# First half's exponentials, convolution order, six experts in halves, and ten constants of an instruction planner

## The chip, the core and the metric

The kernel runs on one core of one Trainium2 chip. The core has five engines that work side by side and meet only through semaphores: TensorE (matrix products, PE in the profile), VectorE (DVE), ScalarE (ACT, which evaluates functions from a loaded table), GpSimd (POOL), and SyncE (SP), which here issues all transfers. The metric is device time in microseconds. Before the change the median of three runs is 1351.64 us (1351.54 to 1353.74).

## The reference

Eight sequences of 512 tokens with 128 channels go through four residual blocks, each behind a layer norm. All is in fp32.

```
x = x + mamba(norm(x))      # projection, 3-tap convolution, silu, decay scan over 512 steps, projection
x = x + moe(norm(x))        # 8 experts, all computed, weighted by a softmax router
x = x + attention(norm(x))  # 16 heads, chunk mask with 25 columns of left context
x = x + moe(norm(x))        # the same weights again
```

The scan block computes, per token, `delta = clip(softplus(dt))`, `decay = clip(exp(-delta * a))`, `drive = (1 - decay) * tanh(b) * xb`, and then `state = decay * state + drive`, `y = sum(state * tanh(c)) + D * xb`. Its other half of the channels, `zb`, passes by the scan. An expert computes `(silu(x Wg) * (x Wu)) Wd` with an inner width of 512.

## The kernel before

**Work and tiles.** Tokens are the free axis, so a sequence is a tile of 128 x 512. The bulk of the work is the expert stream `ffn_stream` (sequence after sequence, expert after expert, four blocks `f` of 128 inner columns each). For each block there are the products `g`, `u` (into one PSUM bank each), the silu of `g`, the product `h`, its split into two parts `hs` of reduced-precision fp32, and the down products `y`. Each product is made of three matmuls over those parts (`matmul3`). The kernel names tiles as in the trace: `xt` and `tp` are the transposed and normalised input, `lps`, `rps`, `cps` the router, `cwb` the spread expert weights, `mh`, `mv`, `mxb`, `mzb`, `mbc`, `mde`, `mdec`, `mst`, `mcx`, `mo` the steps of the scan block in order, `acc` the experts' sum (and, as `macc`, `delta` of the scan block).

**The order.** Nothing of the order is left to a scheduler on the chip. A planner in the same file (classes `Clock`, `Lanes`, `Engine`) walks through Python generators while it builds the program, keeps an estimated end time for each engine, and emits the instructions one by one; each engine then runs its own in that order. The expert stream goes on whenever its inputs and a PSUM bank are free; the other work (scan block of later sequences, router, attention) sits in lanes that are slipped in between. The constants decide when: `SIDE`, `JOIN`, `JOIN_MAX` are the time that a ready piece of TensorE work is held back so that it can go together with another one, `PRESS`, `SECOND`, `FIRST` are advantages in the choice of the next lane, `MAMBA_DUE`, `PREP_DUE`, `LATE` say from which position of the stream a lane counts as late, `WARM_GAP` and `WARM_TO` rule the filler products below.

**The start.** The stream can't begin before sequence 0 has gone through the whole scan block. So this sequence is done in two halves of 256 tokens (`first_halves`): `half(c)` does the convolution and the silu, `scanned(c)` the rest. Within it run the lanes `rows` (tanh, spread products), `inputs`, `decays` (exponentials, which need another ScalarE table than silu and tanh), `clips`, `steps` (scan). In the kernel before, `decays` waits until both halves have had their tanh and silu (`issued["tanh"] == 2`), so the table is changed once for both. `undisturbed` holds the second half's VectorE work while the first half's norm is under way (`"quiet" in done`). `mamba_consts` prepares weights; its last part (`wxz`, and `route_consts`) waits for `"halves" in done`. The expert weights arrive at the same time: ScalarE casts each (`wg`, `wu`, `wd`), GpSimd makes the low part.

**Halves of experts.** For sequence 0, `passes` puts the first `SPLIT` experts on the first half of the tokens, then the same experts on the second half, and the rest on whole sequences. A half product has 256 columns and two `f` blocks share one bank.

**Filler.** While TensorE has nothing to do, the planner emits products that nobody reads: `warm` before the stream, `idle` in it (`keep_warm`, up to position `WARM_TO` of the stream, counted in sequences). An `idle` product takes a PSUM bank from the stream's pool and gives it back.

Of the kernel before, what the change touches and what calls it, by code (L numbers as in the profile page):

```python
# [93 lines left out]
AHEAD = 0.2  # L94
EDGE = 0.1
FIRST = 0.6
LATE = 0.3
SIDE = 0.5
JOIN = 2.0
JOIN_DUE = 0.0  # L100
JOIN_MAX = 6.0
JOIN_ATT = 3.0
JOIN_END = 2.0
MOST = 6
OTHERS = 4
AT_FIRST = 7
WARM = 3.5
WARM_GAP = 0.25
WARM_TO = 1.5
SECOND = 0.2  # L110
PRESS = 0.4
HELD = 0.18
MAMBA_DUE = 0.9
PREP_DUE = 0.9
ATT_LEAD = 2.5
EARLY = 5
SPLIT = 4
EARLIEST = 2 * (DEPTH + 1)


# [257 lines left out]
def block_kernel(ctx: ExitStack, tc: tile.TileContext, x, pack_a, pack_b, pack_c, w_qkv, mask, mask_t, w_o,  # L378
# [24 lines left out]
    done = {}  # L403
# [30 lines left out]
    def freed(t, who="others"):  # L434

        held[who] -= 1
        lanes.give("bank", t + TO_PE)
        return t
# [134 lines left out]
    def mamba_consts(sb, mc):  # L573
        table("natural_log_exp_and_others", 6)

        pick = sb.tile([P, L], F32, tag="dec", name="pick", bufs=5)[:, : 2 * DSTATE]
        pool.tensor_tensor(pick, ident[:, : 2 * DSTATE], ident[:, 32 : 32 + 2 * DSTATE], ALU.add)
        sel = sb.tile([P, 2 * NSTEP, 2, INNER], F32R, name="sel", bufs=1)
        for m in range(2):
            rows = pick[:, m * DSTATE : m * DSTATE + DSTATE].rearrange("p (s i) -> p i s", s=2)  # L580
            pool.tensor_copy(
                sel[:, m * NSTEP : m * NSTEP + NSTEP], rows[:, :, :, None].to_broadcast([P, NSTEP, 2, INNER])
            )
        mc["sel"] = sel.rearrange("p n s c -> p n (s c)")
        yield "A", pa_there

        nega = sb.tile([P, NSTEP], F32, name="nega", bufs=1)
        alog = pa[:, A_ALOG : A_ALOG + NSTEP]
        sp_ = sb.tile([P, NSTEP], F32, tag="sp_a", name="sp_a", bufs=1)
        act.activation(sp_, alog, AF.Abs)  # L590
        act.activation(sp_, sp_, AF.Exp, scale=-1.0)
        act.activation(sp_, sp_, AF.Ln, bias=1.0)
        win = [sb.tile([P, P], F32R, name=f"win_{i}", bufs=1) for i in range(2)]
        src = pa[:, A_WIN : A_WIN + P]
        act.copy(win[0], src)
        yield "V"
        dve.scalar_tensor_tensor(sp_, alog, 0.0, sp_, ALU.max, ALU.add)
        dve.tensor_scalar(nega, sp_, 1e-4, -1.0, ALU.add, ALU.mult)
        dve.tensor_tensor(win[1], src, win[0].bitcast(F32), ALU.subtract)
        mc["win"] = win  # L600
        yield "A"

        cap = sb.tile([P, NSTEP], F32, name="cap", bufs=1)
        act.activation(cap, nega, AF.Exp, scale=1e-4)
        table("silu_and_others", 18)

        yield "T", pc_there
        wp = yield from side([P, P], "wdt_ps")
        pe.matmul(wp, pc[:, 0:P], pc[:, P : 2 * P], start=True, stop=True)
        wdt = sb.tile([P, P], F32, name="wdt", bufs=1)  # L610
        yield "A"
        freed(act.copy(wdt, wp))
        mc["wdt"] = wdt

        wbc = sb.tile([P, P], F32, name="wbc", bufs=1)
        yield "P"
        for h in range(2):
            pool.tensor_copy(
                wbc[INNER * h : INNER * h + INNER].rearrange("p (c n) -> p c n", c=4),
                pa[:INNER, None, A_PBC : A_PBC + 32].to_broadcast([INNER, 4, 32]),  # L620
            )
        mc["wbc"] = wbc
        yield "V"
        dve.tensor_scalar(cap, cap, 1.0, None, ALU.min)
        mc["nega"], mc["cap"] = nega, cap

        yield lambda: "halves" in done
        yield "AV"
        wxz = sb.tile([P, P], F32, name="wxz", bufs=1)
        act.activation(wxz[:INNER], pa[:INNER, A_WOUT : A_WOUT + P], AF.Copy, scale=pa[:INNER, A_D : A_D + 1])  # L630
        mc["wxz"] = wxz, act.copy(wxz[INNER:], pa[INNER:, A_WOUT + P : A_WOUT + 2 * P])
        route_consts()
# [72 lines left out]
    def first_halves(sb, consts, h, xo):  # L705
# [9 lines left out]
        issued = {"tanh": 0}  # L715
        add = first, second

        def half(c):
            cs = slice(c * HALF, c * HALF + HALF)
            v, xb = vs[c], xbs[c]  # L720
            yield "A"
            act.activation(v, h[:, cs], AF.Copy, scale=kc[1])
            yield "V"
            n = 1 - c
            dve.scalar_tensor_tensor(
                v[:, n:], h[:, cs.start + n - 1 : cs.stop - 1], kc[0], v[:, n:], ALU.mult, ALU.add
            )
            yield "V"
            e = dve.scalar_tensor_tensor(
                v[:, : HALF - c], h[:, cs.start + 1 : cs.stop + n], kc[2], v[:, : HALF - c], ALU.mult, ALU.add  # L730
            )
            if c:
                freed(e)
            yield "A"

            act.activation(xb[0:INNER], v[0:INNER], AF.Silu)
            there2 = act.activation(xb[INNER:P], v[0:INNER], AF.Silu)
            yield "T", there2
            pde, pbc = yield from sides(([P, HALF], f"mde0_{c}"), ([P, L], f"mbc0_{c}"))
            pbc = pbc[:, :HALF]  # L740
            pe.matmul(pbc, consts["wbc"][:INNER], xb[:INNER], start=True, stop=True)
            pe.matmul(pde, consts["wdt"][INNER:], xb[INNER:], start=True, stop=True)
            add[c](scanned(c, pbc, pde))

        def scanned(c, pbc, pde):
# [3 lines left out]
            def rows():  # L749
                yield "A"  # L750
                bc = sb.tile([P, L], F32R, tag="bc", name=f"mbc0_{c}")[:, :HALF]
                act.activation(bc, pbc, AF.Tanh)
                act.activation(pbc[32:64], pbc[32:64], AF.Tanh)
                there["z"] = act.activation(zb, vs[c], AF.Silu)
                issued["tanh"] += 1
                yield "V"
                e = freed(dve.tensor_tensor(bc[32:64], pbc[32:64], bc[32:64].bitcast(F32), ALU.subtract))
                for m, into in enumerate((bxs, ccs)):
                    if m:
                        yield lambda: issued["tanh"] == 2  # L760
                    for p in range(2):
                        yield "T", e
                        t = yield from side([P, 2, HALF], f"m{'bc'[m]}x0_{c}_{p}")
                        for i in range(2):
                            into["t", p] = spread(t[:, i], consts, bc, 2 * p + i, m)
                        into[p] = t
# [16 lines left out]
            def decays():  # L783
                yield "V"

                e = freed(dve.tensor_scalar(delta, pde, bdt, LN_E_1, ALU.add, ALU.min))
                yield lambda: issued["tanh"] == 2
                yield "A", e
                nega = consts["nega"]
                table("natural_log_exp_and_others", 6)  # L790
                act.activation(delta, delta, AF.Exp)
                act.activation(delta, delta, AF.Ln, bias=1.0)
                for p in range(2):
                    yield "A"
                    dec = sb.tile([P, 2, HALF], F32, tag="dec", name=f"mdec0_{c}_{p}", bufs=5)
                    for i in range(2):

                        decs["t", p, i] = act.activation(
                            dec[:, i], delta, AF.Exp, scale=nega[:, 2 * p + i : 2 * p + i + 1]
                        )  # L800
                    decs[p] = dec
                if c:
                    table("exp_and_others", 0)
# [53 lines left out]
            for p in range(2):  # L857
                yield lambda: p in scans
                yield from undisturbed()
                yield "V", max(scans[p][1], ccs["t", p])  # L860
                cx = sb.tile([P, 2, HALF], F32, tag="acc", name=f"mcx0_{c}_{p}")
                e = freed(dve.tensor_tensor(cx, ccs[p], scans[p][0], ALU.mult))
                yield "T", e
                for t in range(2):
                    for i in range(2):
                        pe.matmul(
                            ops[t], cx[:, i, t * P : (t + 1) * P], pa[:, A_WOUT : A_WOUT + P],
                            start=False, stop=(p == i == 1),
                        )
            yield "V"  # L870
            part = xo[0][:, 2 * c : 2 * c + 2]
            for t in range(2):
# [150 lines left out]
    def ffn_prep(k, b, xc, t0=0, nt=NT):  # L1023
# [42 lines left out]

        yield lambda: clock.table in TABLES[AF.Exp] or pos[0] >= k * B + b - LATE
        yield "A"
# [351 lines left out]
    def attention(sb):  # L1420
# [62 lines left out]
        def scores(s, both):  # L1483

            qs, ks, _ = loaded[s]
            for m in range(NPAIR):
                for h in range(2):
                    rows = slice(64 * h, 64 * h + QROWS)
                    for i, (q, k) in enumerate(blocks(steps[s][1])):
# [4 lines left out]
                        )  # L1494
            lanes.add(maxima(s, both, e), joins=JOIN_MAX)

# [364 lines left out]
```

## Time and profile before

| | |
|---|---|
| median of three runs | 1351.64 us |
| profiled execution | 1351.62 us, of it a span of 1349.8 us |
| TensorE busy | 1328.9 us |
| VectorE, ScalarE, GpSimd busy | 1036.8, 964.7, 940.4 us |
| first product `g` of the expert stream | 34.31 us after the span's start |
| `ACT_TABLE_LOAD` | 109 records, 1283 ns each |
| mean granted TensorE clock | 0.996 |

The page gives busy times of engines over the span, then a picture of the span in 40 slices, the chain that ended last, and groups of instructions. A line of the timeline has start and duration in us, the engine, the operation with its output and inputs, a count where several were merged, and in brackets how long the engine had been idle and what ended that. A line of the table by stretches has the length of the stretch and then busy time and instruction count of PE, PEld (weight loads), DVE, ACT and POOL, then the granted TensorE clock (1.00 is full), and the share and rate of the transfers. TensorE products are pipelined, so one record is longer than the distance from its start to the next one's.

### The profile page before, as it was taken

To read this page: it belongs to the slowest core of one execution; us is meant where nothing else is said; L and a number is where in the kernel's file an instruction comes from. 1 tells how busy PE (TensorE), PEld (TensorE's weight loads), DVE (VectorE), ACT (ScalarE), POOL (GpSimd) and SP (SyncE) were. 2 spreads that over 40 slices of the span, in tenths; PEclk is the share of its full clock that TensorE was granted. 3 is DMA by queue.
4 is the path that set the end of the run, shared out by engine and by line. 5 is a ranking of instruction groups with operands and counts; after the bars stand their busy time and mean duration, and the time that the engine had idled before them with its cause. 6 is when DMAs were issued, how large, how long until landed. Compare 5 with 4: busy or idle time off the path is not lost.

```text
span 1349.8 us, 29533 instructions
## 1 busy us (share of the span) xinstructions
PE 1328.9 (98%) x10261; PEld 1053.3 (78%) x10261; DVE 1036.8 (77%) x3114; ACT 964.7 (71%) x1694; POOL 940.4 (70%) x1042
## 2 busy tenths in 40 slices
PE   7999999999999999999999999999999999999998
PEld 7877778788788877777777777777777777778887
DVE  6887888688888867898788887888888787855443
ACT  7768576867787556777777777777877767765654
POOL 5877576776767757666766767767677676777776
PEclk9999999999999999999999999999999999999999
DMA  3321304232112242344345444454544434222111
GB/s 126 95 72 38 87 24 101 62 81 73 45 48 56 63 85 54 73 97 118 79 103 111 99 106 100 104 109 89 118 91 104 119 71 88 61 69 55 40 40 40
DMA packets 230861, 107.75 MB, mean 80 GB/s; under 512 B 86417, under 2 KB 226616, under 8 KB 230712
## 3 DMA queue, kind: packets, MB, share of 16 engines
q1 hardware_dynamic: 230712, 105.87, 33.9%
q8 instruction: 81, 1.33, 0.4%
q14 instruction: 68, 0.56, 0.1%
HBM read 77.64 MB, written 27.79 MB: 78 GB/s over the span
## 4 chain that ended last, share of the span: by engine, by line
PE 89%; POOL 3%; ACT 3%; issue 3%; DVE 2%; DMA 0%; POOLq 0%; DVEq 0%
PE u L269 25%; PE y L269 25%; PE g L269 25%; PE ao L269 2%; PE aw L269 2%; PE as L269 2%; POOL h L269 1%; PE mo L269 1%; PE aqk L269 1%; ACT h L269 1%; DVE h L269 1%; PE mde L269 1%; PE aout L269 1%; PE yp L269 1%; ACT L269 1%
## 5 line engine op out<-in xcount | busy, mean ns | idle before, releaser
L269 POOL TENSOR_TENSOR h<-h,h 128x512 fp32r<-128x512 f32 x492 | 640.0, 1310 | 279.0 <-ACT h L269 219.4
L269 PE MATMUL u<-xt_f,wu 128*128 128x512 f32 (+1 forms) x1584 | 451.5, 395 | 3.5 <-ACT h L269 2.7
L269 PE MATMUL g<-xt_f,wg 128*128 128x512 f32 (+1 forms) x1584 | 448.3, 393 | 2.1 <-ACT h L269 1.9
L269 PE MATMUL y<-h,wd 128*128 128x512 f32 (+1 forms) x1584 | 445.5, 392 | 1.4 <-POOL h L269 0.8
L269 DVE TENSOR_TENSOR h<-u,h 128x512 f32<-128x512 f32 x420 | 285.9, 686 | 157.5 <-PE u L269 109.3
L269 ACT ACTIVATE h<-g 128x512 f32<-128x512 f32 x512 | 303.4, 597 | 123.2 <-PE g L269 100.1
L269 ACT CAST h<-h 128x512 fp32r<-128x512 f32 x437 | 268.4, 619 | 171.2 <-DVE h L269 169.6
L269 PEld LDWEIGHTS g<-xt_f,wg 128*128 128x128 f32 x1584 | 288.5, 189 | 70.3 <-ACT h L269 3.0
L269 PEld LDWEIGHTS y<-h,wd 128*128 128x128 f32 x1584 | 288.3, 188 | 70.2 <-POOL h L269 1.4
L269 PEld LDWEIGHTS u<-xt_f,wu 128*128 128x128 f32 x1584 | 286.6, 189 | 71.7 <-ACT h L269 4.1
L269 POOL TENSOR_TENSOR acc<-acc,cwb 128x512 f32<-128x512 f32 (+1 forms) x114 | 148.0, 1298 | 52.5 <-DVE cwb L269 33.8
L269 ACT ACT_TABLE_LOAD x109 | 139.8, 1283 | 24.7 <-PE g L269 23.2
L269 DVE CUSTOM_DVE_ANT_0 amasked<-as,maskq 128x60 f32<-128x60 f32 x640 | 95.4, 213 | 5.0 <-PE as L269 4.8
L269 DVE TENSOR_TENSOR cwb<-y,cwb 128x512 f32<-128x512 f32 (+1 forms) x116 | 77.5, 668 | 16.0 <-PE y L269 14.4
L269 DVE TENSOR_TENSOR apt<-aw,maskk 125x400 f32<-125x400 f32 (+2 forms) x160 | 88.1, 570 | 0.0
L269 DVE SCALAR_TENSOR_TENSOR h<-h,g 128x512 f32<-128x512 f32 x92 | 62.3, 681 | 27.0 <-ACT h L269 26.6
L269 ACT ACTIVATE apt<-apt 125x400 f32<-125x400 f32 (+2 forms) x160 | 81.5, 540 | 0.4
L269 DVE SCALAR_TENSOR_TENSOR h<-u,h 128x512 f32<-128x512 f32 x92 | 62.6, 683 | 3.3 <-PE g L269 0.5
L269 DVE DVE_READ_ACCUMULATOR2_ANT amx<- 128x1 f32 x640 | 52.1, 81 | 0.0
L269 DVE CAST h<-h 128x512 fp32r<-128x512 f32 x75 | 48.8, 651 | 1.2
L269 DVE COPY v<-avr 125x128 f32<-125x128 f32 (+2 forms) x40 | 25.7, 644 | 26.4 <-PE ao L269 26.4
L269 PEld LDWEIGHTS ao<-apt,v 125*32 125x32 f32 (+2 forms) x1280 | 27.4, 109 | 14.6 <-DVE h L269 4.4
(205 smaller groups left out, 1239.5 us busy)
## 6 DMA issues: line engine op xcount, KB each, us to landing
cwb<-cwd_f SPq DMA_DIRECT2D x124, 256.0 KB
aqd<-apc SPq DMA_DIRECT2D x32, 192.0 KB
ks<-aqd SPq DMA_DIRECT2D x48, 93.8 KB
x_fo<-x SPq DMA_DIRECT2D x16, 256.0 KB
aqd<-apc SPq DMA_DIRECT2D x32, 128.0 KB
x_f<-x SPq DMA_DIRECT2D x15, 256.0 KB
qs<-aqd SPq DMA_DIRECT2D x48, 75.0 KB
aod<-aos SPq DMA_DIRECT2D x24, 100.0 KB
```

Source lines behind the costliest of these rows:

```text
L269: f(*args, **kw)
```

## The change

The exponentials of half `c` now wait only for this half's tanh and silu. The second half's convolution on VectorE is emitted after the first's. The late constants wait for `"rows"`, which is set when a half has emitted its tanh and silu. The quiet phase, which holds back the second half's VectorE work, is opened already when the first half's output products have been emitted. `SPLIT` goes from 4 to 6, and ten constants of the planner get other values. Since the planner reads these, the order of the whole program is planned anew.

```diff
-LATE = 0.3
-SIDE = 0.5
-JOIN = 2.0
+LATE = 0.4
+SIDE = 0.6
+JOIN = 3.5
-JOIN_MAX = 6.0
+JOIN_MAX = 8.0
-WARM_GAP = 0.25
-WARM_TO = 1.5
-SECOND = 0.2
-PRESS = 0.4
+WARM_GAP = 0.15
+WARM_TO = 2.5
+SECOND = 0.1
+PRESS = 0.2
-MAMBA_DUE = 0.9
-PREP_DUE = 0.9
+MAMBA_DUE = 1.1
+PREP_DUE = 0.7
-SPLIT = 4
+SPLIT = 6
...
-        yield lambda: "halves" in done
+        yield lambda: "rows" in done
         yield "AV"
         wxz = sb.tile([P, P], F32, name="wxz", bufs=1)
...
             act.activation(v, h[:, cs], AF.Copy, scale=kc[1])
             yield "V"
+            if c:
+                yield lambda: "conv" in issued
+                yield "V"
             n = 1 - c
...
             if c:
                 freed(e)
+            issued["conv"] = 1
             yield "A"
...
                 issued["tanh"] += 1
+                done["rows"] = 0.0
                 yield "V"
...
                     if m:
-                        yield lambda: issued["tanh"] == 2
+                        yield lambda: issued["tanh"] > c
...
                 e = freed(dve.tensor_scalar(delta, pde, bdt, LN_E_1, ALU.add, ALU.min))
-                yield lambda: issued["tanh"] == 2
+                yield lambda: issued["tanh"] > c
                 yield "A", e
...
+            if c == 0:
+                done["quiet"] = 0.0
             yield "V"
             part = xo[0][:, 2 * c : 2 * c + 2]
```

## The prediction

> **What bounds the kernel now.** I read the page first. TensorE is busy for 98% of the span and carries 89% of the chain that ended last, in equal parts for g, u and y: the expert stream.
>
> ```profile
> span 1349.8 us, 29533 instructions
> PE 1328.9 (98%) x10261; PEld 1053.3 (78%) x10261; DVE 1036.8 (77%) x3114; ACT 964.7 (71%) x1694; POOL 940.4 (70%) x1042
> ...
> PE 89%; POOL 3%; ACT 3%; issue 3%; DVE 2%; DMA 0%; POOLq 0%; DVEq 0%
> ```
>
> So time can only come from three places: the 34.31 us before the first g, the waits inside the stream, and work added to or taken from TensorE. The timeline of the start shows the first. The change of tables at 17.67 stands behind the second half's silu (mzb), the exponentials (macc) begin 1.30 us later, and the first half's transposed input (xt_f) is copied at 32.36.
>
> ```profile
> 14.59 0.40 ACT L269 ACTIVATE mzb<-mv 128x256 f32<-128x256 f32 x1
> 17.25 0.40 ACT L269 ACTIVATE mzb<-mv 128x256 f32<-128x256 f32 x1
> 17.67 1.28 ACT L569 ACT_TABLE_LOAD   x1
> 18.97 0.87 ACT L269 ACTIVATE macc<-macc 128x256 f32<-128x256 f32 x2
> 32.36 0.37 ACT L269 CAST xt_f<-tp_f 128x256 fp32r<-128x256 f32 x1 [2.85 <-PE tp_f L269]
> 34.31 0.77 PEld L269 LDWEIGHTS g<-xt_f,wg 128*128 128x128 f32 x6 [0.26 <-PE idle L269]
> ```
>
> TensorE's timeline in the stream shows the second. Filler (idle) hides part of the waits: five of them fill 68.38 to 70.58, 0.44 us apart, because each waits for the bank of the one before.
>
> ```profile
> 67.25 0.27 PE L269 MATMUL cps_f<-ident,cw_f 128*16 128x128 f32 x1
> 68.38 2.14 PE L269 MATMUL idle<-sel 128*128 128x256 f32 x5 [0.86 <-DVE cwt_f L269]
> 70.58 1.46 PE L269 MATMUL u<-xt_f,wu 128*128 128x256 f32 x6
> ...
> 176.60 1.64 PE L269 MATMUL g<-xt_f,wg 128*128 128x512 f32 x3 [1.94 <-ACT h L269]
> ```
>
> The table by stretches adds what such a wait costs afterwards: the next 3.4 us run at half the clock, which is 1.7 us of work lost. In the stream this happens twice.
>
> ```profile
> 67.40:70.90 3.50, 2.35 (x9) 1.25 (x8) 3.45 (x12) 3.45 (x5) 0.97 (x2) 0.99 0.02 4
> 70.90:74.30 3.40, 3.40 (x15) 3.01 (x14) 2.44 (x7) 3.39 (x8) 2.70 (x5) 0.51 0.26 75
> 173.30:176.70 3.40, 1.46 (x7) 0.85 (x5) 1.25 (x3) 3.37 (x6) 2.25 (x2) 0.99 0.15 38
> 176.70:180.10 3.40, 3.40 (x8) 2.71 (x9) 2.37 (x4) 2.06 (x4) 1.86 (x2) 0.51 0.17 39
> ```
>
> In both, ScalarE is full (3.45 of 3.50, 3.37 of 3.40): it changes tables and makes decays while TensorE waits for a silu to free a bank.
>
> The sum is made against the profiled execution, 1351.62 us (span 1349.8 and 1.8 around it), practically the median of 1351.64.
>
> **A. The start, up to the first g.** The instruction order of the changed program tells what moves; rows of before give durations.
> ScalarE: the two wxz copies (9.56 to 10.27) move from before the convolution to behind mzb; mh ends at 9.91, so the convolution's first copy goes from 10.30 to 9.95, and all of half 0 with it (0.35). The convolution's order on VectorE and ScalarE is the same in both programs: that edit moves nothing. The first mzb then ends at 14.64, wxz at 15.3, the table load (1.30) at 16.6: the first exponentials come 2.4 us earlier than 18.97. But ScalarE then has in its queue: macc 0.87, decays 1.71, a load back 1.30, the second half's silus 0.84, 0.82 until its tanh (TensorE products between, filled by a weight cast), tanh and mzb 1.1, six weight casts or small copies 2.2, a load 1.3, macc 0.9, decays and two casts 2.8, a load 1.3. Two loads are new. That is 31.8 for the xt copy instead of 32.36; the router and the two products mo follow (0.41 and 0.71), and the filler at 33.95 before g is gone: g at 33.5, **-0.8 us**. VectorE and GpSimd would allow earlier: mcx of half 0 ends at 24.5 (26.89 less 2.4), the norm's power waits on GpSimd behind three weight parts to 28.9, tp ends at 30.0. So the 2.4 us become 0.8, because ScalarE is next late. Bounds: -2.4 (ScalarE not in the way) and +1.0 (one more wait of the kind before macc).
>
> The Trainium skill, "ScalarE: Activation LUTs", section "What ACT_TABLE_LOAD costs", puts a switch at 1.28 us plus a drain of about 1.38, 2.66 in all, and so speaks against this change. The row decides: the next activation starts 1.30 us after the load. By the page the three loads behind 16.6 would put xt 4.1 us later, and the whole sum at about 1352.
>
> **B. From g to the end of expert 3's first half.** A common mark is the product mde of sequence 1, with the same 15.1 us of expert products before it in both orders; before, it starts at 57.05. The quiet phase now holds back the second half on VectorE: in the old order two mbx products and two clips (0.69, 0.41, 0.69, 0.90) ran before the xt part at 33.04; in the new one all of it comes after. From 32.98: mbx 0.69 twice, a copy 0.27, clips to 35.4 (they wait for GpSimd's 1.3 us part, as the 0.90 us clip at 29.48 did), scans 1.37 each, two mcx 0.68, with silu steps between. mcx ends at 40.6 and 44.5, against 37.47 and 39.67. Behind them in TensorE's queue stand mo, then cps (0.27, GpSimd's weight at 46.1), then the fourth g: at about 46.3 instead of 41.97. Allowing for what was reordered, expert 2's first u is 4.5 us behind. Then the old order has what the new one lacks: seven more filler products there (14 against 7), standing for 0.4, 1.0 and 1.1 us of waiting at 45, 51.7 and 56.0, and small ones. The new chain goes over GpSimd's parts (h of expert 1 at 52.6) and seven groups of 0.72 to mde at 57.4, or over the convolution and silu to 55.9. I take the later, 57.3: **A and B together +0.2 us**. Bounds: -1.2 and +4.5 (nothing caught up).
>
> **C. From there to sequence 1** (before: g at 129.06). I sum the waits of before: 3.2 (67.3 to 70.6), 1.7 half clock, 1.1, 0.75, 0.55, 0.9, and about 1.5 in small ones at 117 to 129: 9.7 us, of which 14 fillers at 0.31 (9.25 us for 30 in the stream) are 4.3. Between two silus of the stream ScalarE has at most so much other work, priced by rows (copy 0.53, decay 0.65, load 1.30): before 5.9, 7.0, 5.5 and 6.4 us, in the new order once 8.2 (six experts in halves put sequence 1's decays and the router's exponential under one pair of loads; from the mark on the old order has eight loads, the new one four with the pair on the border to sequence 1). So: again 14 fillers, 4.3; other waits 3.7 x 8.2/24.8 = 1.2; one half clock with even chance 0.85. Sum 6.4, **-3.3 us**. Bounds: -6 (no half clock, short fillers) and +2 (a wait of 8.2 less the 5 that pass unnoticed, with a half clock).
>
> **D. Later sequences.** Waits of before: 1.6 at 150, 1.94 and 1.7 (half clock) at 175, 1.45 at 264, 0.7 at 521, 0.84 at the end: 8.3 us. ScalarE's gaps over 5.6 us number five before and eight after, the largest 7.0 and 7.2. Filler now goes on to position 2.5, which keeps the clock up in a wait like that at 175 but costs 0.12 to 0.44 each. I take half of one half clock away, **-0.9**; bounds -4 and +4, since the new order's waits can't be read from the old trace.
>
> The Trainium skill, "TensorE: Matmul & The Clock Gate", section "HAM oscillation — how this bites in real kernels", asks only for no TensorE gaps above about 3.4 us. Here a wait of 1.94 us, busy 1.46 in the window, was enough. By the page D would hold no half clock at all, and its -0.9 would be -1.7.
>
> **E. TensorE's own work.** 144 products of 256 columns replace 72 of 512: 12 of them take 1.44 us (61.75 to 63.19 on TensorE), 0.12 each, and three of 512 columns 0.70 (704.74 to 705.44), 0.23 each. 144 x 0.120 - 72 x 0.2315 = **+0.6 us**. The products slipped into the stream leave it 261 times instead of 273; two more of the small transposes of attention go with a neighbour, which the rows price at 0.08 each: **-0.2** (0 to -1). The four extra transfers and GpSimd additions lie beside the stream.
>
> Sum: +0.2 - 3.3 - 0.9 + 0.6 - 0.2 = -3.6: **1348.0 us**.
>
> **Rivals.**
> *R1, VectorE's late second half is never made up* (slower). Place: TensorE's queue at mo, 37 to 50 us. For it: the 4.5 us behind, and VectorE busy for 8.9 of the 10 us from 40 to 50, so it has little to catch up with. Against it: the gaps of before that follow. Price: +4.5 for B and a half clock of 1.7: 1351.6 + 4.5 + 1.7 - 3.3 - 0.9 + 0.4 = 1354.0, and 1357.3 where C gains nothing; the middle is 1355.5. It decides when mde starts later than about 61.
> *R2, the waits only move.* For it: 33 fillers against 30, ScalarE's gaps over 5.6 add up alike. C and D are 0: 1351.6 + 0.2 + 0.4 = 1352.2, or 1350 with the start's bound. The early exponentials do not do what they say, since ScalarE meets the same 31.8.
> *R3, both half clocks and half of the later waits go.* C -6, D -4: 1351.6 + 0.2 - 10 + 0.4 = 1342.
>
> **How the numbers follow.** Forecast 0.52 (own range 1344 to 1351.5; about 0.7 of it below 1348.9), R1 0.22, R2 0.10, R3 0.16. A difference below 0.2% (2.7 us) can't be told from none. Faster: 0.36 + 0.16 + 0.02 = 0.54; same 0.21; slower 0.25. The range leaves a tenth at each side: half of R3 below 1342, half of R1 above 1355.5.
>
> **What would show it.** In the changed kernel: a table load near 15.3 and exponentials near 16.6; xt_f's copy right behind a load near 31.9, g near 33.5 (A); TensorE waiting for DVE mcx near 38 to 45, mde near 57 (B); one long ScalarE run before expert 5 with fillers and perhaps a clock of 0.5, and g of sequence 1 near 126 (C). I am wrong if g of sequence 1 starts after 129, or if waits beyond 130 us add up to more than 12 us.

## The result and the profile after

The changed kernel takes 1368.65 us (median of five, 1364.74 to 1369.59) against 1351.54 (1350.17 to 1353.74) before: the ratio is 1.0119, with an interval of 1.0101 to 1.0137. It is 17 us slower. The forecast was 1348.0, its range ended at 1355.5. The profiled execution of the changed kernel took 1364.74 us, the least of the five, so the two traces differ by 13.2 us of span (1363.0 against 1349.8); the sums below are made against that, and some 4 us of the loss are in no trace.

The head of the page and the chain that ended last, of the changed kernel:

```profile
span 1363.0 us, 29691 instructions
...
PE 1336.1 (98%) x10328; PEld 1059.4 (78%) x10328; DVE 1036.8 (76%) x3103; ACT 964.3 (71%) x1708; POOL 942.0 (69%) x1046
...
PE 85%; ACT 5%; DVE 4%; DMA 2%; issue 1%; POOL 1%; SPq 1%; POOLq 0%; DVEq 0%; ACTq 0%
```

All engines are busy for as long as before to within 0.7%. What changed is the chain: 85% of it is TensorE instead of 89%, and transfers, 0% before, have 2%. Of the 13.2 us TensorE counts as idle for 6.0 and as busy for 7.2; fillers that stand in a wait and products at half the clock also count as busy, so the page alone doesn't separate waiting from work. The timeline of the start shows that the time didn't go there:

```profile
15.55 1.28 ACT L569 ACT_TABLE_LOAD   x1
16.85 0.86 ACT L269 ACTIVATE macc<-macc 128x256 f32<-128x256 f32 x2
...
32.12 0.37 ACT L269 CAST xt_f<-tp_f 128x256 fp32r<-128x256 f32 x1
33.60 0.78 PEld L269 LDWEIGHTS g<-xt_f,wg 128*128 128x128 f32 x6
33.63 0.96 PE L269 MATMUL g<-xt_f,wg 128*128 128x256 f32 x6
```

The load was forecast for 15.3, the exponentials for 16.6, the copy for 31.8 and the first g for 33.5. The list of what TensorE waited for (in total, times, longest, from the first g to the end) shows some of the new waits; the first fence is the changed kernel, the second the kernel before:

```profile
PE u L269 <- DVE h L269: 3.5, 2, 2.3
PE idle L269 <- DVE mst L269: 2.7, 2, 1.4
PE idle L269 <- ACT h L269: 2.5, 2, 2.0
PE idle L269 <- DVE s_f L269: 1.5, 2, 1.3
...
PE as L269 <- DMA ks<-aqd: 0.6, 1, 0.6
```

```profile
PE u L269 <- ACT h L269: 2.7, 3, 1.4
PE g L269 <- ACT h L269: 1.9, 1, 1.9
PE idle L269 <- DVE cwt_f L269: 0.9, 1, 0.9
...
PE avt L269 <- DVE h L269: 0.2, 1, 0.2
```

The first line of the changed kernel has a wait of 2.3 us for a product h on VectorE, near 1064 us; between 690 and 1140 us TensorE's longest wait before was 0.2 (the last line). The third has 2.0 us for a silu. The table by stretches shows what such waits cost behind them (columns as in the prediction: length, PE, PEld, DVE, ACT, POOL, granted clock, transfers):

```profile
78.80:82.20 3.40, 1.39 (x9) 1.19 (x10) 3.19 (x6) 1.62 (x3) 2.18 (x3) 1.00 0.73 190
82.20:85.60 3.40, 3.40 (x17) 3.30 (x17) 1.78 (x3) 0.44 (x1) 2.30 (x3) 0.50 0.03 7
133.40:136.80 3.40, 1.94 (x9) 1.18 (x8) 3.07 (x6) 2.82 (x5) 0.51 (x2) 1.00 0.00 0
136.80:140.20 3.40, 3.40 (x10) 2.65 (x9) 2.69 (x4) 0.00 (x0) 0.81 (x1) 0.50 0.05 14
```

Twice a stretch with TensorE busy for 1.39 or 1.94 of 3.40 us is followed by one at half the clock; with one near 38 us these are three in the stream, before it was two.

**The plan as a second clock.** The order is laid by a planner that keeps an estimated time for every instruction, and each engine runs its list in that order. So the n-th product in the plan can be set beside the n-th TensorE record of the trace, and the difference tells where the chip falls behind. Planned start, start on the chip, and the difference (us) at some products:

```
                       before                    after
first g              37.6    34.3   -3.3       35.5    33.6   -1.9
mde of sequence 1    62.4    57.1   -5.3       59.4    57.6   -1.8
g of sequence 1     132.2   129.0   -3.2      126.0   128.3   +2.3
g of sequence 2     213.7   213.1   -0.6      213.3   217.4   +4.1
g of sequence 4     371.1   371.8   +0.7      374.1   379.5   +5.4
second pass         690.6   692.7   +2.1      690.0   699.0   +9.0
  its sequence 4   1033.7  1037.9   +4.2     1034.5  1049.1  +14.6
end of TensorE     1343.8  1345.7   +1.9     1344.8  1358.8  +14.0
```

Two things are to be read here. In the plan itself the changed kernel reaches sequence 1 6.2 us earlier, loses 5.8 in sequence 1, and ends 1.0 later: the waits moved, they did not go (in the plan, waits and fillers of sequence 0 fall from 17.9 to 13.0 us and those of sequence 1 rise from 3.7 to 9.5). And the chip then falls 11.7 us behind from sequence 1 to the end, where before it fell 5.1 behind.

These are single executions, and the start scatters. Up to the first g five kernels of this document share the list of before, planned for 37.6, and six share that of the changed kernel, planned for 35.5. In their traces the first g came at 34.31, 35.02, 35.52, 36.49 and 37.28 us, and at 32.79, 32.93, 33.63, 34.84, 34.92 and 34.98. The trace of before is the earliest of its list, and a difference of 1 or 2 us between two traces at the start says little.

### The profile page after: what moved, and what is told of

Same layout as the page of the kernel before. It is cut to its first block, busy times and chain, and to the rows that moved or that the text cites. A ratio compares the mean times of both kernels' runs of the same rounds, so it can differ in the third digit from the quotient of the medians.

```text
span 1363.0 us, 29691 instructions
## 1 busy us (share of the span) xinstructions
PE 1336.1 (98%) x10328; PEld 1059.4 (78%) x10328; DVE 1036.8 (76%) x3103; ACT 964.3 (71%) x1708; POOL 942.0 (69%) x1046
## 4 chain that ended last, share of the span: by engine, by line
PE 85%; ACT 5%; DVE 4%; DMA 2%; issue 1%; POOL 1%; SPq 1%; POOLq 0%; DVEq 0%; ACTq 0%
PE u L269 24%; PE g L269 23%; PE y L269 23%; PE ao L269 2%; PE aw L269 2%; PE as L269 2%; ACT h L269 1%; DVE h L269 1%; PE mo L269 1%; ACT L269 1%; SPq L269 1%; PE warm L269 1%; PE aqk L269 1%; PE idle L269 1%; PE yp L269 1%
```

## The experiments

Three theories stood at the start. T1: the ten constants carry the loss. T2: the second half's lateness at the start does (rival R1 of the prediction). T3: any list laid anew comes out several us away, whatever was edited. Each run is listed with the planner's estimate of its end.

**One part at a time.** First the code edits alone (old constants, `SPLIT = 4`), then `SPLIT` alone, the ten constants alone, and all but the ten constants.

```diff
-SPLIT = 4
+SPLIT = 6
```

> The kernel before with only the edits to the start (the two waits on both tanhs become waits on the own half, the second half's convolution waits for the first's, the constants of the output projection wait for the first half's row), four experts in halves and the ten old constants of the order. T1 (the ten constants carry the loss in the later sequences; the start does what the trace of after shows, 0.7 us earlier): 1350 to 1352. T2 (the second half's lateness at the start is never made up): 1360 or more. T3 (any list that the planner lays anew comes out several us away, up or down, whatever was edited): anywhere from 1345 to 1370, and the sum of the parts does not give the whole.

> The kernel before with six experts in halves instead of four and nothing else. T1: about 0.6 us for the 144 products of 256 columns in place of 72 of 512, so 1351.5 to 1354. T2: not decisive, 1352 to 1355. T3: anywhere from 1345 to 1370, although only 72 of some ten thousand products are cut.

> The kernel before with the ten constants of the order at their new values, and neither the edits of the start nor six experts in halves. T1: 1361 to 1367, with the added waits and bare switches in sequences 1 to 4 and 7 to 12. T2: 1350 to 1354. T3: anywhere from 1345 to 1370.

> The changed kernel with the ten constants of the order at their old values: the edits of the start and six experts in halves stay. T1: 1349 to 1353, the sum of the two alone. T2: 1362 or more. T3: anywhere, and not the sum of start alone and halves alone.

Measured: 1377.89 us, ratio 1.0178 (1.0162 to 1.0193), for the edits of the start; 1360.78, 1.0055 (1.0038 to 1.0071), for the halves; 1377.90, 1.0180 (1.0157 to 1.0204), for the ten constants; 1365.77, 1.0097 (1.0077 to 1.0117), for all but the constants. By the ratios the parts alone add up to some 56 us, and together they cost 16. T1 had 1361 to 1367 for the ten constants alone and at most 1354 for the parts without them, and T2, which fits the start alone and the run without the constants, had no loss for the halves or the constants alone (1352 to 1355, 1350 to 1354): so both are out. T3 had said that the parts would not add up, but its range ended at 1370, below two of the four. The planner's own ends explain much of it: 1361.0, 1351.7, 1362.9 and 1352.8, against 1344.5 for before and 1345.5 for the changed kernel.

**A nudge that changes no work.** One constant of the kernel before was moved by 3% down, then by 3% up.

```diff
-PRESS = 0.4
+PRESS = 0.388
```

```diff
-PRESS = 0.4
+PRESS = 0.412
```

> The kernel before with one constant of the order moved by 3% (PRESS 0.400 to 0.388); no work is added or taken. The planner's own estimate of the end goes from 1344.5 to 1342.3, and it lays the list anew from sequence 1 on. In the first four runs the time stood 13 to 17 us above the planner's estimate (9 with six halves alone), before stands 7 above its own. T3 (any new list loses, because the list of before happens to fit the chip and its neighbours do not): 1351 to 1359, slower or at best equal although the planner thinks it shorter. T1 (the values of the ten constants or the edits matter as such, a nudge does not): 1349 to 1353.

> The kernel before with the same constant moved by 3% the other way (PRESS 0.400 to 0.412). The planner's estimate is 1358.1, 13.6 above that of before. T3: the planner's loss is real and the distance comes on top, 1366 to 1375. T1: a nudge of 3% is nothing, 1349 to 1354. A third reading, that the planner's estimates mean nothing on the chip: no more than 1360.

Measured: 1347.41 us, ratio 0.9964 (0.9951 to 0.9977), and 1366.00, 1.0103 (1.0088 to 1.0118). The plans were 1342.3 and 1358.1. So a nudge of 3% without any meaning is worth -4.8 or +14 us, as much as the whole change, and the planner foresees most of the larger one (13.6) and less than half of the other (2.2). T3 was wrong in one point: the lower nudge beat the kernel before instead of losing. T1, for which a nudge is nothing, was wrong in both. The head of the page and the chain of that run:

```profile
span 1346.5 us, 29546 instructions
...
PE 1327.6 (99%) x10261; PEld 1052.5 (78%) x10261; DVE 1032.7 (77%) x3109; ACT 967.0 (72%) x1701; POOL 937.5 (70%) x1040
...
PE 92%; ACT 3%; DVE 2%; DMA 1%; issue 1%; POOL 1%; SPq 0%; POOLq 0%; DVEq 0%; ACTq 0%
```

It has the same 10,261 products as the kernel before, TensorE on 92% of the chain, and no stretch at half the clock inside the stream.

**Where the distance of the changed kernel arises.** The ten constants go back to their old values when the stream reaches position 5, so that sequences 0 to 4 keep the changed order and the attention part gets another.

```diff
                         pos[0] = k * B + b + (n * NFC + f + n_chunks - 1) / (len(todo) * NFC)
+                        if pos[0] >= 5:
+                            globals().update({"LATE": 0.3, "SIDE": 0.5, "JOIN": 2.0, "JOIN_MAX": 6.0, ...})
```

> The changed kernel, whose ten constants go back to their old values when the stream reaches position 5 (sequences 0 to 4 are ordered as in the changed kernel; planner's end 1344.1 against 1345.5). If the new constants are at fault in the attention part (the trace of after has about 7.7 us more lost time there than before): 1357 to 1361. If what was re-planned carries the loss whatever the constants: 1364 to 1369, no gain.

Measured: 1360.63 us, ratio 1.0069 (1.0051 to 1.0086), 7 to 8 less than the changed kernel; the plan accounts for 1.4 of that. From the first g of the second pass to that of its sequence 6 TensorE fell behind the plan by 2.9 us here, by 8.2 in the changed kernel and by 2.7 before. So some 5 to 6 us of the loss come from how the attention part was laid. The run lies in the range that blames the new constants there; but the kernel with the ten constants alone also fell behind by only 2.6 in that stretch, so their values as such don't do it in every list.

**Transfers that come late.** VectorE's queue stood 11.0 us waiting for transfers in the changed kernel, 3.1 before. Here two kinds of them land where nobody waits, so that the result lacks the routing weights and the division of the attention.

```diff
-                        state["cwb", (k, b, e, cs.start)] = cwb, sp.dma_start(
-                            out=cwb.rearrange("p (t q) -> p t q", q=P),
+                        land = dram.tile([P, L], F32, name=f"land{k}_{b}_{e}_{cs.start}")[:, :n]
+                        state["cwb", (k, b, e, cs.start)] = cwb, sp.dma_start(
+                            out=land.rearrange("p (t q) -> p t q", q=P),
...
-            t = freed(dve.tensor_tensor(cwb, y, cwb, ALU.mult), "experts")
+            t = freed(dve.tensor_tensor(cwb, y, wgt['d', 0][0][:, cs].bitcast(F32), ALU.mult), "experts")
...
-            dve.reciprocal(over, over)
+            dve.reciprocal(over, wgt['d', 0][0][:, : L // HD].bitcast(F32))
```

> The changed kernel with the same list of instructions on every engine, but two kinds of transfers land where nobody waits for them: the expert weights spread over the partitions (cwb) and the sums of the attention (aover) go to a scratch in DRAM, and VectorE takes other resident numbers in their place (the routing weights and the division thus leave the result). In the trace of after VectorE's queue stands 11.0 us waiting for transfers, 8.2 of them for these two, against 3.0 before. T4 (transfers land later than planned, VectorE's queue stands behind them, and the stream behind VectorE): 4 to 8 us off, 1358 to 1364. T5 (these waits lie beside the stream): 1366 to 1369.

Measured: 1368.40 us, ratio 1.0117 (1.0102 to 1.0132): nothing gained. At the place of the worst wait (1062 us) TensorE no longer stood for h, but right there the next instruction in VectorE's queue met the next transfer:

```profile
DVE x_fo L269 <- DMA x_fo<-x: 2.9, 1, 2.9
```

In all VectorE still stood 7.3 us for transfers, and the clock fell to half four times in the stream instead of three. So T4's 4 to 8 us are not there; but only 3.7 us of such waits were taken away on balance, and this run alone doesn't show that they cost nothing. A later run says more (the kernel before with one wait told to its planner, below): 18.1 us of such waits, and no slower than before.

**Two waits by themselves.** The comparison of plan and chip had two sharp steps. Near 80 us, in the timeline of the changed kernel:

```profile
77.55 1.29 POOL L269 TENSOR_TENSOR wd<-staged,wd 128x512 fp32r<-128x512 f32 x1
...
78.80 1.27 POOL L269 TENSOR_TENSOR h<-h,h 128x512 fp32r<-128x512 f32 x1
...
80.10 0.60 ACT L269 ACTIVATE h<-g 128x512 f32<-128x512 f32 x1 [2.07 <-POOL h L269]
...
80.75 0.38 PE L269 MATMUL idle<-sel 128*128 128x256 f32 x1 [2.00 <-ACT h L269]
```

The silu at 80.10 writes into one of three buffers h, and the low part that GpSimd makes at 78.80 still reads it. The planner had set that silu before the end of the low part: `hidden` waits until the low part has been emitted (`ends.pop(("lo", i - 3), None)`), but never takes its end into account. All engines had run a steady 1.3 us ahead of the plan up to here; the silu came 1.55 us too late, TensorE stood 2.00, and the half clock at 82.20 follows. Near 1062 us:

```profile
1062.71 1.33 SPq L269 DMA_DIRECT2D aover<-aod  x2
...
1065.52 0.55 DVE L269 RECIPROCAL aover<-aover 128x64 f32<-128x64 f32 x1 [3.18 <-DMA aover<-aod]
...
1065.99 0.63 DVE L269 SCALAR_TENSOR_TENSOR h<-u,h 128x512 f32<-128x512 f32 x1
...
1066.67 0.50 PE L269 MATMUL u<-xt_f,wu 128*128 128x512 f32 x1 [2.31 <-DVE h L269]
```

VectorE's division stands at the head of its queue and waits 3.18 us for a transfer; the product h of the stream is behind it, and TensorE behind that. The transfer was issued 3.5 us later against the plan than the other engines ran. SyncE was already 2.3 us later than they were when it issued aod at 1055.60, and that issue took 1.84 us instead of the planned 0.55 (the last section). This run moves only these two instructions in their queues; the rest of every list stays.

```
GpSimd:   wd(6) low part, h(expert 5) low part   ->   h(expert 5) low part, wd(6) low part
VectorE:  division of aover(5), h, 16 amasked and apt, h   ->   h, 16 amasked and apt, h, division of aover(5)
```

> The changed kernel with the same list on every engine but for two moves. On GpSimd the low part of expert 6's wd and the low part of h of expert 5 change places, so that the silu behind them (ScalarE, near 80 us, 2.07 us of waiting for GpSimd) finds its buffer free; on VectorE the division of aover of sequence 5 moves behind the next two products h (near 1062 us, where VectorE stands 3.18 us for that transfer). All is computed as before. T6 (these two waits, which the planner's clock does not know, are each carried to the end: TensorE stands 2.5 us further behind the plan after the first, with its half clock, and 2.6 after the second): 1362 to 1365, and no half clock near 82. T5 (lateness at such a place is absorbed later, or the next wait in the queue takes its place): 1367 to 1370.

Measured: 1362.43 us (1358.08 to 1367.69), ratio 1.0071 (1.0049 to 1.0092) against 1.0119 (1.0101 to 1.0137) for the changed kernel: about 6 us by the medians for two moved instructions, within the range of T6 (each of the two waits is carried to the end), though the six executions lie 9.6 us apart. In the trace of that run the silu at 83.02 still waits, but for less, and no half clock follows:

```profile
83.02 0.60 ACT L292 ACTIVATE h<-g 128x512 f32<-128x512 f32 x1 [1.40 <-POOL h L292]
...
83.67 0.38 PE L292 MATMUL idle<-sel 128*128 128x256 f32 x1 [0.59 <-ACT h L292]
```

```profile
81.80:85.20 3.40, 2.75 (x20) 2.22 (x20) 3.40 (x7) 1.63 (x3) 3.40 (x3) 1.00 0.44 121
```

Around the second place TensorE has no wait left at all, and the division costs nobody anything:

```profile
1069.44 0.69 DVE L292 TENSOR_TENSOR h<-u,h 128x512 f32<-128x512 f32 x1
1070.05 0.54 DVE L292 RECIPROCAL aover<-aover 128x64 f32<-128x64 f32 x1
```

From the g of sequence 4 to that of sequence 6 of the second pass the distance grew by 0.1 us here, by 2.6 in the changed kernel. The profiled execution (1365.80) is longer than the median of its six: it has half clocks at 45, 76, 138 and 220 us, three of them at places where the changed kernel has the same list and had none. From the first g to the g of sequence 1 TensorE fell behind by 4.2 us, as in the changed kernel (4.1). So the first move's gain is not seen in this trace, the second's is.

**A planner that knows the wait.** The missed wait for GpSimd is told to the planner, once for the changed kernel and once for the kernel before; further constants are nudged so that the planned end is a good one.

```diff
-                yield lambda: ends.pop(("lo", i - 3), None)
+                yield lambda: ("lo", i - 3) in ends
+                there = max(there, ends.pop(("lo", i - 3)))
```

> The changed kernel, whose planner is told one wait that it left out: the silu writes into one of three buffers h and cannot start before GpSimd has read the one of three products earlier. The list is planned anew (JOIN_ATT 3.09; planner's end 1346.3). T6: the distance between time and estimate falls from 23 (19 in the profiled execution) to 10 to 14, so 1356 to 1360. If the distance is chance: 15 to 25, so 1361 to 1371.

> The kernel before with the same wait told to its planner (SIDE 0.45, HELD 0.1908; planner's end 1344.6, as before without it). T6: distance 4 to 9 as in before or less, 1349 to 1353.5. If the good fit of before is chance and any new list loses it: 1355 to 1365.

Measured: 1362.24 us, ratio 1.0067 (1.0053 to 1.0081), a distance of 16 from its plan, where T6 had 10 to 14; and 1352.18, 0.9995 (0.9985 to 1.0004), a distance of 7.6. The first is a miss for T6 and lies in the range of chance: knowing one wait was not enough. VectorE stood 25.1 us for transfers in it and the clock was halved near 43 and 74 us, but that these are the reason is not shown. The second shows that a list laid anew need not lose.

**The best plan near the kernel before.**

```diff
-SECOND = 0.2
+SECOND = 0.212
-LATE = 0.3
+LATE = 0.27
-MAMBA_DUE = 0.9
+MAMBA_DUE = 0.927
```

> The kernel before with three constants of the order moved by 3 to 10% (SECOND 0.212, LATE 0.27, MAMBA_DUE 0.927), chosen because the planner's estimate of the end, 1341.1, is the lowest of 150 such kernels; before has 1344.5. T3b (the planner's estimate is right up to a distance, and lists near that of before keep its distance of 5 to 8): 1346 to 1349, faster than both kernels. T3 (a list chosen by its estimate alone brings a larger distance, as that of the changed kernel does): 1351 to 1362.

Measured: 1350.67 us (twelve runs), ratio 0.9978 (0.9968 to 0.9988): faster than both kernels. It lies between T3b's range and T3's: of the 3.4 us that the plan gained, 3.0 arrive by the ratio and 2.0 by the medians of the same session.

**Each edit with a good list.** Last, the edits were given lists with a planned end near that of before: 1344.0 (both edits, `JOIN` 2.12, else old constants), 1348.6 (the start alone), 1347.0 (the halves alone), 1342.6 (the changed kernel, `ATT_LEAD` 2.75, `HELD` 0.198). The first differs from the fourth run above by one line:

```diff
-JOIN = 2.0
+JOIN = 2.12
```

> The edits of the start and six experts in halves, with the old constants but JOIN 2.12 for 2.0 (planner's end 1344.0 against 1352.8 without that nudge, which took 1365.8 on the chip). If the edits themselves cost distance (13 to 16 in three lists that have both): 1357 to 1360. If the distance belongs to ill-fitting lists and this one fits as before does: 1350 to 1353.

> The edits of the start alone, four experts in halves, four constants moved by 3 to 10% (planner's end 1348.6 against 1361.0 of the start alone). If the edits of the start carry distance (17 in the start alone): 1362 to 1366. If it is the halves that carry it, or nothing does: 1355 to 1357.5.

> Six experts in halves alone, three constants moved by 3 to 10% (planner's end 1347.0 against 1351.7). The halves alone had 9 of distance, 4 of it gained in sequence 0, where all lists with six halves fall 4 to 5 us behind the plan, and lists with four halves up to 2.3. If the halves carry that: 1355 to 1358. If not: 1352 to 1354.5.

> The changed kernel with two of its other constants moved by 10% (ATT_LEAD 2.75, HELD 0.198), planner's end 1342.6, the lowest of 150 neighbours; the start's list is the same until the attention begins. If the distance at the start stays (5 in sequence 0, 9 by the second pass) and the attention fits like that of before (about 3): 1355 to 1358. If the new constants spoil the fit of the attention whatever the list: 1360 to 1366.

Measured: 1353.88 us, ratio 1.0015 (1.0006 to 1.0024); 1363.34, 1.0081 (1.0066 to 1.0096); 1363.34, 1.0077 (1.0060 to 1.0095); 1361.48, 1.0067 (1.0051 to 1.0082). The first decides about the code edits and the halves: they are the same as in the changed kernel, and with the old constants and another list they are 14 us faster by the ratios, within 0.2% of before and 1 us above the range for a list that fits. So these edits needn't cost anything. They don't bring a gain in this list either: its first g is at 32.7 us and g of sequence 1 at 126.4, as forecast, and by the g of sequence 2 (212.3 against 213.1) little is left. The other three stand 15 to 19 us above their plans, although their plans were better than those of the lists they replace. The start alone fell into the range that blames the edits of the start, which the first run contradicts. The halves alone lie 5 us above both of their ranges, and with a plan 4.7 us better took 2.6 us more than without: a better plan is no promise. The changed kernel fell into the range "the new constants spoil the fit of the attention whatever the list", and no run here rules out that they have a part in it.

**All runs together.** Planned end, median time, the difference, and stretches of 3.4 us at half the clock inside the stream of the profiled execution:

```
before             1344.5  1351.5   7.0  2     press lower        1342.3  1347.4   5.1  0
after              1345.5  1368.7  23.2  3     press higher       1358.1  1366.0   7.9  3
start alone        1361.0  1377.9  16.9  4     before, told       1344.6  1352.2   7.6  0
halves alone       1351.7  1360.8   9.1  1     three nudges       1341.1  1350.7   9.6  0
constants alone    1362.9  1377.9  15.0  3     both, JOIN 2.12    1344.0  1353.9   9.9  1
all but constants  1352.8  1365.8  12.9  2     start, nudged      1348.6  1363.3  14.7  3
old from 5         1344.1  1360.6  16.5  4     halves, nudged     1347.0  1363.3  16.3  3
two moves          1345.5  1362.4  16.9  4     after, nudged      1342.6  1361.5  18.9  3
after, told        1346.3  1362.2  15.9  2     transfers aside    1345.5  1368.4  22.9  4
```

The planned end is that of VectorE's last instruction. The time is the planned end plus 5 to 23 us. With none or one half clock the distance is 5 to 10, with two 7 to 16, with three or four 14 to 23 (the higher PRESS, 7.9, is the exception). That is a correlation, with the half clocks of one execution beside the median of several: each half clock costs only 1.7 us, and what the rest is made of is not shown. All seven lists that have the ten new constants, in whole or up to position 5, stand 15 or more above their plan (three of them are nearly the same list); of the eleven with the old ones nine stand below 15. So a part of the distance may belong to the new constants. A list that has them and fits its plan was not found, and the question stays open.

## Why the prediction was wrong

**Step A held.** First g at 33.63 us, forecast 33.5, before 34.31. The Trainium skill, "ScalarE: Activation LUTs", section "What ACT_TABLE_LOAD costs", asks 2.66 us for a change of table; in the changed kernel the exponentials follow the load at 15.55 by 1.30 us, and the three further loads did not push the copy of xt back; as the step said, that copy comes right behind a load. The size was met by this pair of traces, partly by luck: over the executions with the same start (above) the first g comes 1.7 us earlier, 34.0 instead of 35.7, where the step had 0.8.

**Step B held.** The mark mde of sequence 1 started at 57.59, forecast 57.3. In four other executions with the same list up to there it came at 56.9 to 60.5, so none reached 61, where rival R1 would have decided. VectorE's late second half is not what made the kernel slower.

**Step C was 2 us too hopeful.** The g of sequence 1 came at 128.26 instead of 126: -0.75 against before (129.00 in the row; the prediction has 129.06) where A to C gave -3.1. The plan itself has 126.0; the chip fell 2.5 us behind it at the silu near 80, with the half clock that the step had given an even chance.

**Step D is the one that failed.** It said "-0.9; bounds -4 and +4, since the new order's waits can't be read from the old trace". From the g of sequence 1 to the end the changed kernel took 13.8 us longer than before (1230.5 against 1216.7), with E in it. By the table above that is 7.2 us which the plan itself has more (5.8 of it in sequence 1, where the waits of sequence 0 went: what rival R2 called "the waits only move") and 6.6 of distance, 5.2 of them in the second pass. The step took the old waits as the budget and asked how much of it would go. But a list laid anew has waits of its own. The step's budget was 8.3 us, of which it left 7.4. Behind 130 us TensorE's gaps above 0.15 us add up to 11.4 us after and 5.9 before, twelve fillers that stand in waits take 5.1 where two took 0.9, and a half clock has 1.7 in both: 18.2 us by the step's own count. Some 4 us more are spread over small distances between products and are not singled out. The bounds of 4 us had no row behind them. The runs give one: nudges of 3% and single parts moved the time by -4.8 to +24 us.

**Step E**, +0.4 in all, is too small to be seen apart; it lies inside the 13.8.

**Of the rivals** none had the mechanism whole. R2 had the plan's half, and put it at 0 instead of +1. The distance between plan and chip had no rival. The condition "waits beyond 130 us add up to more than 12 us" came true with these 18.2 us; the other one did not, since g of sequence 1 started before 129. The missing case was "the list laid anew fits the chip less well than the one before", with its place (any queue where an instruction of other work stands ahead of the stream's), its price (by these runs up to 16 us more than the 7.0 of before) and the point from which it decides (4 us, the whole hoped-for gain). What remains open is why one list fits and another doesn't, and whether the ten constants have a part in it: two waits, moved together, are worth some 6 us by the medians, of which a trace shows 2.5 at the second; the others are only counted. And that the list before fits well because it was picked by measuring is a guess that no run here tests.

## What to carry to other kernels

Where a planner or scheduler lays the whole order, a change of a few lines is a change of every queue. Before forecasting it, take the planner's estimate for both versions and for some meaningless nudges: their spread is the uncertainty, and an expected gain smaller than it is no forecast at all. Then set plan beside trace, look for the places where the chip falls behind for good, and ask which wait the planner doesn't know. Here one nudged constant gave 1347.41 us, faster than either kernel, and the best plan of 150 gave 1350.67.

## What the runs showed of the hardware that was not expected

**The same list is not halved at the same places.** Four runs have the same list from the start to position 5, but for the experiments' own edits. Their half clocks in the stream began at 37.8, 82.2, 136.8 (changed kernel); 36.9, 81.3, 135.9, 217.8 (old from 5); 45.4, 76.1, 86.4, 219.5 (transfers that nobody waits for); 45.5, 76.3, 137.7, 219.6 (two moves). Each lasts 3.4 us. In each of the eighteen traces the clock changes only at steps of 3.413 us, and where these steps lie differs from trace to trace: 0.25 us after the span's start and then every 3.413 us in the changed kernel, 2.57 us after it in the kernel before. Cut along these steps, the streams of the eighteen traces have 6849 stretches at full clock. All nine with TensorE busy for less than 1.7 us were followed by a stretch at half the clock, 30 of the 99 with 1.7 to 2.6 us, and none of the 6741 with more. So a wait of 1 to 2 us is a chance of losing 1.7 us, and it depends also on how it falls on the steps. Times of one kernel vary too (the two moves ran from 1358.08 to 1367.69), but the half clocks of the one trace don't tell by how much: the three nudges, with none, ran from 1347.38 to 1352.57, and the told changed kernel, with two, from 1361.36 to 1362.56. The Trainium skill, "TensorE: Matmul & The Clock Gate", section "HAM oscillation — how this bites in real kernels", warns of gaps above about 3.4 us; here gaps of 2.00 and 1.34 us came before a half clock.

**Issuing a transfer can take three times as long.** On SyncE the same transfer was issued in 0.56 to 1.84 us (shortest, median, longest in ns):

```profile
L269 SPq DMA_DIRECT2D aod<-aos x40: 563/577/1844, 552.2 to 1200.3; - x40
```

The longest came at 1055.60, ahead of the late aover in SyncE's queue. In the eighteen traces the longest of the forty lies between 1.09 and 3.56 us. The planner has 0.55 for each.
